# A two-layer graph-attention kernel: where three steps at the start stand, and how the last pairs' units are shared out

## The chip, the cores and the metric

The kernel runs on one core of one Trainium2 chip (trn2). The metric is the device time of one execution in microseconds, as a median over runs. Everything is float32.

## The reference, cut to what matters

There are 64 graphs of 256 nodes with 512 features each, one adjacency matrix of 256 x 256 for all of them, and two layers with a residual each:

```python
h = relu(layernorm(x))
q, k, v = h @ Wq + bq, h @ Wk + bk, h @ Wv + bv            # 8 heads of 64
s = q k^T / 8 + (1 - adj) * -1e9                           # per head
x = x + (softmax(s) @ v) @ Wo + bo
h = relu(layernorm(x))
g = h @ W
e = leaky_relu(g a1 + (g a2)^T, 0.2) * adj
x = x + elu(softmax(e) @ g + beta * g)
```

## The kernel before, in words

**Pairs and units.** The graphs are worked in 32 pairs (`NP`). A product of a pair with a 512 x 512 weight is done with seven block products instead of eight, in the manner of Strassen and Winograd: two graphs by two halves of the features make the four blocks of one operand, and sums and differences of blocks make up the rest. One such product is a `Unit`; its seven block products are issued by `u.p(i)` in the order 1, 4, 6, 2, 7, 5, 3, and `products(u, ...)` adds the step that writes results: `put11` after p2, `put2` after p5, `put12` after p3. Each block product is eight recorded matmuls on TensorE. Between the products VectorE makes running sums out of PSUM: `u2` after p6 (L262), `u3` after p7 (L265). The units are `UnitQK` (two for each pair, L317), `UnitV` (`v_p`), `UnitO` (`o_p`, the output projection) and `UnitW` (`w_p`, the second layer's weight). `p2` and `p3` add to the banks of p1 and p5, so p3 cannot start before `put2` has read p5's bank.

**Block sums.** Three functions make the sums of the activations that a unit needs: `combine_31` (two of them, on POOL for o in `o_blocks`, L435, on VectorE for h and z), `combine_2` (L281, needed by p6) and `combine_4` (L285, needed by p3). The tiles of o are called s_o in the profile, those of z s_z.

**Layer 0.** `scores(b, q)` makes four heads' scores of graph b on TensorE (L393); ScalarE takes the exponential (L397), POOL multiplies by the mask (L398) and adds the two halves (L400), 128 x 512 and 128 x 256 at a time. `values(b, q)` multiplies by v (`av`, L411), makes the sums of the softmax (`sm`, L420), and VectorE does the reciprocal (L422), adds to a check sum and writes oT (L426 follows on POOL, put off to a later place by `between`). `residuals(p)` loads x again through SyncE's queue into y (L442) and adds bo and a constant on POOL (L443). `UnitO` adds into y.

**Layer 1.** `y_stats`, `y_scales`, `y_normal` make the layer norm into h2; `y_sums` multiplies h2 by two rows derived from W and a (`pr`, L486, on VectorE); `gat_scores` turns the sums into rows on TensorE (`pe`, L160) and makes e; `gat_exp`, `divide`, `gat_t` (transposes `at`, L519, copied to eT at L520), `gat_z` (`pz`, L533), and `UnitW` with elu: m on ScalarE (L553, L554), o on VectorE (L556), and `finish`, which adds m to o on the engine that it is given (L562) and stores it.

**Order.** `tc.manual_schedule` holds TensorE, VectorE, ScalarE and POOL to the order in which the program is written, and each engine's queue runs in that order: an instruction that waits holds all behind it on its engine. The order is written out in `start` (pair 0), `first` (pair 1, first part), `first_half(p)` and `second_half(p, uo)` for pairs 1 to 30, `last` (pair 31's attention, with unit o_30 and w_29) and `end` (the rest: w_30, o_31, w_31). In the middle, one pair of every kind is worked in each round: o of the pair before, w of the one before that, v and qk of the next.

**Buffers.** PSUM has eight banks under one name. SBUF tiles have a tag with a number of buffers:

```python
BUFS = {"set": 13, "qk": 8, "v": 4, "pt": 4, "xt": 4, "y": 8, "e": 2, "eT": 2, "m": 2, "c": 3, "u": 4}
```

`pr` and the o of elu share the three buffers of "c"; h2 has two of 128 x 2 x 512.

**Small setup.** `project_b` loads Wo, makes its four sums (L116 to L119), and adds bv @ Wo to bo: four columns of bv spread over 128 x 128 (`bvb`, L176, two buffers) and 16 recorded matmuls (`pbo`, L179). It is called between v_0's p5 and p3. `project_a` does the same kind of thing for W; its last part is the product `pwa` (L160).

Of the kernel before, what the change touches and what calls it, by code (L numbers as in the profile page):

```python
# [16 lines left out]
P = 128  # L17
# [6 lines left out]
def kernel(ctx: ExitStack, tc: tile.TileContext, x, adj, wq, bq, wk, bk, wv, bv, wo, bo, w, a, beta, out):  # L24
# [33 lines left out]
    BUFS = {"set": 13, "qk": 8, "v": 4, "pt": 4, "xt": 4, "y": 8, "e": 2, "eT": 2, "m": 2, "c": 3, "u": 4}  # L58
# [103 lines left out]
    def project_b():  # L162

        WO, b12, sums = weight("wo", wo, True)
        sums()
        nc.sync.dma_start(bo2, bo.partition_broadcast(P))
        bvc = sb([P, DC], "bvc", "bvc", 1)
        with nc.allow_non_contiguous_dma(reason="a bias, once"):
            bv_v = bv.rearrange("(q i s d) -> i d q s", q=2, i=4, s=2, d=HH)
            for i in range(4):  # L170
                for q in range(2):
                    nc.sync.dma_start(bvc[i * HH:(i + 1) * HH, 2 * q:2 * q + 2], bv_v[i, :, q, :])
        ps = bank("pbo")
        for c in range(DC):
            cb = sb([P, P], "rec", f"bvb_{c}")
            nc.vector.tensor_scalar(cb, ones, bvc[:, c:c + 1], None, ALU.mult)  # L176
            for f in range(2):
                b = ((WO[1], b12), (WO[2], WO[3]))[c // 2][f]
                nc.tensor.matmul(ps[:, f * N:(f + 1) * N], cb, b[:, c % 2, :], start=(c == 0 and f == 0),  # L179
                                 stop=(c == DC - 1), skip_group_check=True)  # L180
        nc.vector.scalar_tensor_tensor(bo2, bo2, -1.0, ps, op0=ALU.add, op1=ALU.add)
        return WO
# [256 lines left out]
    def residual(p, gi, fh):  # L439
        g = 2 * p + gi  # L440
        r = Y[g, fh] = blk("y", f"y_{g}_{fh}")
        nc.sync.dma_start(r, x[g].rearrange("(t p) c -> p t c", p=P)[:, :, fh * N:(fh + 1) * N])  # L442
        nc.gpsimd.tensor_tensor(r, r, bo2[:, fh * N:(fh + 1) * N].unsqueeze(1).to_broadcast([P, 2, N]), ALU.add)  # L443
# [31 lines left out]
    def normal(g, rstd, nmr):  # L475
        h2 = H2[g] = sb([P, NT, D], "h2", f"h2_{g}")
        SC[g] = sb([P, NT, 2], "s12", f"s12_{g}", 3)
        for t in range(NT):
            for f in range(2):
                nc.scalar.activation(h2[:, t, f * N:(f + 1) * N], Y[g, f][:, t, :], AF.Relu, bias=nmr[:, t:t + 1],  # L480
                                     scale=rstd[:, t:t + 1])

    def node_sums(g, t):
        for j in range(2):
            pr = sb([P, D], "c", f"pr_{g}_{t}_{j}", BUFS["c"])
            nc.vector.scalar_tensor_tensor(pr, H2[g][:, t, :], 1.0, war[:, j, :], op0=ALU.mult, op1=ALU.mult,  # L486
                                           accum_out=SC[g][:, t, j:j + 1])
# [33 lines left out]

    def gat_z(p):
        s = blocks(("z", p), f"z{p}")
        pss = {}
        for gi in range(2):
            g = 2 * p + gi
            h2, eT = H2.pop(g), ET.pop(g)
            for half in range(2):
                ps = pss[gi, half] = bank(f"pz_{g}_{half}")
                for f in range(2):  # L530
                    fs = slice((2 * half + f) * P, (2 * half + f + 1) * P)
                    for k in range(NT):
                        nc.tensor.matmul(ps[:, f * N:(f + 1) * N], h2[:, k, fs], eT[:, k, :],  # L533
                                         start=(k == 0), stop=(k == NT - 1))
                dst = blk("set", f"z_{g}_{half}")
                nc.scalar.copy(dst, two(ps))  # L536
                s[BLOCK[2 * gi + half]] = dst
# [4 lines left out]
        combine_31(s, of(pss[1, 0]), of(pss[1, 1]))  # L542

    class UnitW(Unit):
# [5 lines left out]
        def elu(self, gi, fh, src, o=None):  # L550
            g = 2 * self.pair + gi
            m = blk("m", f"m_{g}_{fh}")
# [22 lines left out]
        def put12(self):  # L575
            nc.vector.tensor_tensor(two(self.b), two(self.b), self.u2, ALU.add)
            self.elu(0, 1, two(self.b))

# [51 lines left out]
    def residuals(p):  # L630
        for gi, fh in ((0, 0), (1, 1), (1, 0), (0, 1)):
            residual(p, gi, fh)
# [6 lines left out]
    def start():  # L639
# [36 lines left out]
        products(uv, 4, 6, 2, 7, 5)  # L676
        wo_blocks = project_b()
# [3 lines left out]
    def first():  # L681
# [37 lines left out]
        products(uv, 6)  # L719
        combine_2(A["o", 0])  # L720
        products(uv, 2)
        x_normals(2, *range(2 * NT))
        products(uv, 7)
        combine_4(A["o", 0])
        products(uv, 5)
        prods(5)
        products(uv, 3)
        uo = UnitO(0)
# [39 lines left out]
    def second_half(p, uo):  # L768
# [37 lines left out]
        scores(g1 + 1, 0, {1: add})  # L806
        residuals(p)
# [5 lines left out]
        products(uv, 4, 6, 2)  # L813
        if p == NP - 2:
            o_blocks(p, "xt")
        products(uv, 7, 5)
        if p == NP - 2:
            combine_24(A["o", p])
# [4 lines left out]
    def last():  # L823
        p = NP - 1
        g0, g1 = 2 * p, 2 * p + 1
        uo = UnitO(p - 1)
        products(uo, 1, 4, 6, 2)
        y_stats_0(p - 1)
        products(uo, 7, 5)
        add = values(g0, 0)  # L830
        y_stats_1(p - 1)
        products(uo, 3)
        y_stats_2(p - 1)
        scores(g0, 1, {0: lambda: y_scales(p - 1), 1: add})
        uw = UnitW(p - 2)
        products(uw, 1, 4)
        y_normal(p - 1, 1)
        products(uw, 6)
        y_sums(p - 1, 1, 0, 1)
        products(uw, 2)  # L840
        y_normal(p - 1, 0)
        products(uw, 7)
        add = values(g0, 1)
        y_sums(p - 1, 0, 0, 1)
        scores(g1, 0, {1: add})
        gat_scores(g1 - 2)
        gat_exp(g1 - 2)
        uw.p(5)
        gat_scores(g0 - 2)
        gat_exp(g0 - 2)  # L850
        uw.put2()
        uw.finish(0, 0, nc.gpsimd)
        divide(p - 1)
        uw.finish(1, 1, nc.vector)
        products(uw, 3)
        uw.finish(1, 0, nc.vector)
        add = values(g1, 0)
        scores(g1, 1, {1: add})
        uw.finish(0, 1, nc.vector)
        residuals(p)  # L860
        gat_t(g1 - 2)
        gat_t(g0 - 2)
        gat_z(p - 1)
        values(g1, 1)()
        o_blocks(p)

    def end():
        p = NP - 1
        g0, g1 = 2 * p, 2 * p + 1
        z = A["z", p - 1]  # L870
        uw = UnitW(p - 1)
        products(uw, 1, 4)
        combine_24(A["o", p])
        uo = UnitO(p)
        products(uo, 1, 4, 6, 2, 7)
        combine_24(z)
# [5 lines left out]
        normal(g1, rstd, minus(mr, f"y{g1}"))  # L882
        products(uw, 6)
        products(uo, 3)
        y_stats(g0, NT, 0, g0, 1)
        rstd, mr = scales(f"y{g0}", 2)
        y_sums(p, 1, 0, 1)
        products(uw, 2)
        normal(g0, rstd, minus(mr, f"y{g0}"))
        products(uw, 7)  # L890
# [3 lines left out]
        uw.p(5)  # L894
# [3 lines left out]
        gat_t(g1)  # L898
        uw.put2()
        uw.finish(0, 0, nc.gpsimd)  # L900
        gat_divide(ATT[g0], gsums[:, NT * g0:NT * g0 + NT], g0)
        products(uw, 3)
        uw.finish(1, 1, nc.gpsimd)
        gat_t(g0)
        uw.finish(1, 0, nc.gpsimd)
        gat_z(p)
        uw.finish(0, 1, nc.gpsimd)
# [4 lines left out]
        products(uw, 3)  # L912
        uw.finish(1, 1, nc.vector)
        uw.finish(1, 0, nc.gpsimd)
        uw.finish(0, 1, nc.vector)

    with tc.manual_schedule(engines={ENG.PE, ENG.DVE, ENG.Activation, ENG.Pool}):
# [4 lines left out]
        for p in range(2, NP - 1):  # L922
            second_half(p, first_half(p))
        last()
# [31 lines left out]
    def general(src, dst, W, mask):  # L956
# [77 lines left out]
        for f in range(DC):  # L1034
            ps = bank(f"fz_{f}")
            for k in range(NT):
                nc.tensor.matmul(ps[:, :N], h2[:, k, f * P:(f + 1) * P], eT[:, k, :], start=(k == 0),
# [65 lines left out]
```

## Time and profile before

| | |
|---|---|
| median of 3 runs | 2902.8 us (2901.25 to 2905.18) |
| profiled execution, its own time | 2903.83 us |
| its span | 2902.0 us, clock 0.99 |
| TensorE busy | 2852.2 us, 98% |
| VectorE busy | 2063.2 us, 71% |
| POOL busy | 1618.4 us, 56% |
| ScalarE busy | 1046.3 us, 36% |
| one pair in the middle | 88.1 us |
| TensorE without a stop | 175.5 to 2763.5 us |
| TensorE's last product ends | 2892.35 us |

In the profile PE is TensorE, DVE VectorE, ACT ScalarE, POOL GpSimd, SP SyncE. A row of the timeline gives the start, the length, the engine and line, the operation, its output and inputs and, in brackets, how long the engine stood idle before it and what ended that. Matmuls that follow each other without a gap share a row. A line of the waits gives engine, line, what was waited for, and then total us, times and the longest.

### The profile page before, as it was taken

The numbers are of one execution on the slowest core, as the hardware profiler recorded it, in microseconds if no ns is written. First come the engines' busy times: TensorE is split into PE (matmuls) and PEld (weight loads), VectorE is DVE, ScalarE is ACT, GpSimd is POOL, SyncE is SP. The second block draws the span as 40 slices with busy tenths as digits, with TensorE's granted clock in tenths as the row PEclk, the third lists the DMA queues.
The fourth block names the chain that finished last, engine by engine and source line by source line (L and its number), as shares of the span: only waits on it lengthen the run. The fifth ranks groups of instructions, "written<-read, shape, count | busy, mean of one in ns | idle before, by whom it ended". The sixth has DMA issues, their size and how long they took to land.

```text
span 2902.0 us, 46357 instructions
## 1 busy us (share of the span) xinstructions
PE 2852.2 (98%) x18110; PEld 2338.2 (81%) x18110; DVE 2063.2 (71%) x3652; ACT 1046.3 (36%) x2116; POOL 1618.4 (56%) x1588
## 2 busy tenths in 40 slices
PE   8899999999999999999999999999999999999987
PEld 7688888888888888888888888888888888888865
DVE  5567767677767678666677676777676786666765
ACT  2233333334333334333333333343333343333332
POOL 2656555556555565555565555565555655555752
PEclk9999999999999999999999999999999999999998
DMA  5001111001110011110011110011110111100110
GB/s 152 9 15 44 44 45 44 16 30 44 45 44 32 21 37 45 44 44 26 19 44 44 45 44 15 30 45 44 44 32 21 37 44 44 45 26 19 30 30 30
DMA packets 96463, 110.00 MB, mean 38 GB/s; under 512 B 8560, under 2 KB 79472, under 8 KB 96240
## 3 DMA queue, kind: packets, MB, share of 16 engines
q1 hardware_dynamic: 96240, 106.99, 11.8%
q8 instruction: 145, 2.38, 0.4%
q14 instruction: 78, 0.64, 0.1%
HBM read 73.41 MB, written 33.55 MB: 37 GB/s over the span
## 4 chain that ended last, share of the span: by engine, by line
PE 96%; DVE 2%; POOL 1%; issue 0%; ACT 0%; DMA 0%; SPq 0%; DVEq 0%; POOLq 0%; ACTq 0%
PE qk_p L329 27%; PE v_p L362 14%; PE o_p L362 13%; PE w_p L362 13%; PE sc L393 8%; PE av L411 8%; PE pz L533 8%; PE tr L308 2%; PE sm L420 2%; PE at L519 1%; PE pe L160 0%; POOL pt L398 0%; DVE pr L486 0%; PE pbo L179 0%; DMA x<-in_x_dram 0%
## 5 line engine op out<-in xcount | busy, mean ns | idle before, releaser
L398 POOL TENSOR_TENSOR pt<-pt,maskT 128x512 f32<-128x512 f32 x512 | 719.5, 1405 | 601.1 <-ACT pt L397 601.1
L400 POOL TENSOR_TENSOR pp<-pt 128x256 f32<-128x256 f32 x512 | 433.6, 847 | 40.1
L397 ACT ACTIVATE pt<-sc 128x512 f32<-128x512 f32 x512 | 264.4, 603 | 344.9 <-PE sc L393 344.7
L486 DVE SCALAR_TENSOR_TENSOR pr<-h,war 128x512 f32<-128x512 f32 x256 | 303.3, 1228 | 57.2 <-ACT h L480 57.2
L562 POOL TENSOR_TENSOR o<-o,m 128x512 f32<-128x512 f32 x36 | 45.9, 1276 | 512.1 <-ACT m L554 471.1
L393 PE MATMUL sc<-qk 64*128 64x256 f32 x2048 | 255.7, 389 | 0.0
L411 PE MATMUL av<-pt,v 128*32 128x256 f32 x4096 | 250.2, 383 | 2.4 <-POOL pt L398 2.4
L393 PEld LDWEIGHTS sc<-qk 64*128 64x128 f32 x2048 | 187.3, 186 | 69.9 <-PE av L411 37.9
L422 DVE RECIPROCAL rec<-sm 128x256 f32<-128x256 f32 x128 | 223.3, 1745 | 14.5 <-PE sm L420 14.5
L533 PE MATMUL pz<-eT,h 128*128 128x256 f32 x1024 | 228.9, 382 | 2.8 <-ACT eT L520 2.8
L533 PEld LDWEIGHTS pz<-eT,h 128*128 128x128 f32 x1024 | 196.2, 192 | 30.5 <-ACT eT L520 3.4
L411 PEld LDWEIGHTS av<-pt,v 128*32 128x32 f32 x4096 | 120.6, 110 | 112.7 <-issue 33.5
L329 PE MATMUL qk_p<-s_h,wq_t 128*128 128x256 f32 x768 | 197.4, 379 | 0.0
L329 PE MATMUL qk_p<-s_h,wk_t 128*128 128x256 f32 x768 | 197.1, 379 | 0.0
L362 PE MATMUL w_p<-w_t,s_z 128*128 128x256 f32 x768 | 177.9, 381 | 0.0
L362 PE MATMUL v_p<-wv_t,s_h 128*128 128x256 f32 x768 | 176.3, 379 | 0.0
L362 PE MATMUL o_p<-wo_t,s_o 128*128 128x256 f32 x768 | 176.3, 379 | 0.0
L540 DVE TENSOR_TENSOR s_z<-pz,z 128x512 f32<-128x512 f32 x64 | 44.2, 691 | 179.1 <-ACT z L536 179.1
L536 ACT COPY z<-pz 128x512 f32<-128x512 f32 x128 | 74.9, 585 | 254.1 <-PE pz L533 254.1
L362 PEld LDWEIGHTS w_p<-w_t,s_z 128*128 128x128 f32 x768 | 146.6, 191 | 20.1
L362 PEld LDWEIGHTS o_p<-wo_t,s_o 128*128 128x128 f32 x768 | 145.8, 190 | 20.1 <-ACT pt L397 0.3
L362 PEld LDWEIGHTS v_p<-wv_t,s_h 128*128 128x128 f32 x768 | 145.8, 190 | 20.1 <-ACT pt L397 0.3
(167 smaller groups left out, 5728.6 us busy)
## 6 DMA issues: line engine op xcount, KB each, us to landing
x<-in_x_dram SPq DMA_DIRECT2D x128, 256.0 KB, 3.7
y<-in_x_dram SPq DMA_DIRECT2D x128, 256.0 KB, 2.9
out_dram<-o SPq DMA_DIRECT2D x128, 256.0 KB, 2.2
wq_b<-in_L_gnn_Wq_dram SPq DMA_DIRECT2D x4, 256.0 KB, 5.7
wk_b<-in_L_gnn_Wk_dram SPq DMA_DIRECT2D x4, 256.0 KB, 6.2
wv_b<-in_L_gnn_Wv_dram SPq DMA_DIRECT2D x4, 256.0 KB, 5.0
wo_b<-in_L_gnn_Wo_dram SPq DMA_DIRECT2D x16, 64.0 KB, 2.1
w_b<-in_L_gnn_W_dram SPq DMA_DIRECT2D x4, 256.0 KB, 3.4
```

Of the source, the lines that this page charges most:

```text
L308: nc.tensor.transpose(ps[:, c * N + t * P:c * N + (t + 1) * P], XT[g, t][:, f0:f0 + P], ident)
L329: nc.tensor.matmul(ps[:, j * N:(j + 1) * N], wj[i][:, c, ft * P:(ft + 1) * P], s[i][:, c, :], start=(start and j == 0 and c == 0), stop=(c ...
L362: nc.tensor.matmul(ps[:, t * N:(t + 1) * N], s[i][:, c, t * P:(t + 1) * P], wj[i][:, c, :], start=(start and t == 0 and c == 0), stop=(c = ...
L393: nc.tensor.matmul(pss[2 * pair + h][:, k * N:(k + 1) * N], qk[hs, 1, k * P:(k + 1) * P], qk[hs, 0, :], start=True, stop=True)
L397: nc.scalar.activation(pt, two(pss[i]), AF.Exp, scale=QSCALE)
L398: nc.gpsimd.tensor_tensor(pt, pt, maskT, ALU.mult)
L400: nc.gpsimd.tensor_tensor(pp, pt[:, 0, :], pt[:, 1, :], ALU.add)
L411: nc.tensor.matmul(ps[i * HH:(i + 1) * HH, s * N:(s + 1) * N], v[:, k, c0:c0 + HH], pts[i][:, k, :], start=(k == 0), stop=(k == NT - 1))
L422: nc.vector.reciprocal(rec, sums[:, :N])
L486: nc.vector.scalar_tensor_tensor(pr, H2[g][:, t, :], 1.0, war[:, j, :], op0=ALU.mult, op1=ALU.mult, accum_out=SC[g][:, t, j:j + 1])
L533: nc.tensor.matmul(ps[:, f * N:(f + 1) * N], h2[:, k, fs], eT[:, k, :], start=(k == 0), stop=(k == NT - 1))
L536: nc.scalar.copy(dst, two(ps))
```

## The change

Five edits.

1. `project_b` is cut in two calls. The Wo sums are issued after v_0's p6 instead of after p5; the four bvb columns (`shift(0)`) after p7, in two tiles of two columns; the pbo products (`shift(1)`) stay after p5.
2. In `first`, combine_2 and combine_4 of o_0 move from between v_1's products to behind its p3.
3. The end. In `second_half(30)` o_blocks is issued ahead of the residuals, and gat_z(29), v_31's p3 and the combines go into `last`. There, values and scores of pair 31 are put between the parts of units o_30 and w_29; all of o_31 comes in `end`, ahead of the z product of pair 30 and unit w_30; `divide(30)` is later; pair 31's residuals and h2 take buffers of "qk"; more of the finishes are on POOL.
4. w_31's last block (`put12_finish`) is done in two halves, each 128 x 256, with two stores.
5. h2 is two tiles of 128 x 512 with four buffers; `gat_z` is cut into a function for each graph.

```diff
         ps = bank("pbo")
-        for c in range(DC):
-            cb = sb([P, P], "rec", f"bvb_{c}")
-            nc.vector.tensor_scalar(cb, ones, bvc[:, c:c + 1], None, ALU.mult)
-            for f in range(2):
-                b = ((WO[1], b12), (WO[2], WO[3]))[c // 2][f]
-                nc.tensor.matmul(ps[:, f * N:(f + 1) * N], cb, b[:, c % 2, :], start=(c == 0 and f == 0),
-                                 stop=(c == DC - 1), skip_group_check=True)
-        nc.vector.scalar_tensor_tensor(bo2, bo2, -1.0, ps, op0=ALU.add, op1=ALU.add)
-        return WO
+        cbs = []
+
+        def part(n):
+            if n == 0:
+                for c in range(DC):
+                    if c % 2 == 0:
+                        cbs.append(sb([P, 2, P], "rec", f"bvb_{c}"))
+                    nc.vector.tensor_scalar(cbs[-1][:, c % 2, :], ones, bvc[:, c:c + 1], None, ALU.mult)
+                return
+            for c in range(DC):
+                for f in range(2):
+                    b = ((WO[1], b12), (WO[2], WO[3]))[c // 2][f]
+                    nc.tensor.matmul(ps[:, f * N:(f + 1) * N], cbs[c // 2][:, c % 2, :], b[:, c % 2, :],
+                                     start=(c == 0 and f == 0), stop=(c == DC - 1), skip_group_check=True)
+            nc.vector.scalar_tensor_tensor(bo2, bo2, -1.0, ps, op0=ALU.add, op1=ALU.add)
+
+        return WO, part
...
-    def residual(p, gi, fh):
+    def residual(p, gi, fh, tag):
         g = 2 * p + gi
-        r = Y[g, fh] = blk("y", f"y_{g}_{fh}")
+        r = Y[g, fh] = blk(tag, f"y_{g}_{fh}")
...
-    def normal(g, rstd, nmr):
-        h2 = H2[g] = sb([P, NT, D], "h2", f"h2_{g}")
+    def normal(g, rstd, nmr, tag="h2"):
+        h2 = H2[g] = [sb([P, D], tag, f"h2_{g}_{t}", BUFS[tag]) for t in range(NT)]
...
+    def z_graph(p, gi):
+        s = A.get(("z", p)) or blocks(("z", p), f"z{p}")
+        h2, eT = H2.pop(2 * p + gi), ET.pop(2 * p + gi)
+        s["ps"] = []
+        for half in range(2):
+            ps = bank(f"pz_{p}_{gi}_{half}")
+            s["ps"].append(ps)
+            for f in range(2):
+                fs = slice((2 * half + f) * P, (2 * half + f + 1) * P)
+                for k in range(NT):
+                    nc.tensor.matmul(ps[:, f * N:(f + 1) * N], h2[k][:, fs], eT[:, k, :],
+                                     start=(k == 0), stop=(k == NT - 1))
+            dst = s[BLOCK[2 * gi + half]] = blk("set", f"z_{p}_{gi}_{half}")
+            nc.scalar.copy(dst, two(ps))
+
...
+        def put12_finish(self):
+
+            g = 2 * self.pair
+            y, m, o = Y.pop((g, 1)), blk("pt", f"m_{g}_1"), blk("pt", f"o_{g}_1")
+            for t in range(NT):
+                src = self.b[:, t * N:(t + 1) * N]
+                nc.vector.tensor_tensor(src, src, self.u2[:, t, :], ALU.add)
+                nc.scalar.activation(m[:, t, :], src, AF.Relu, scale=-1.0)
+                nc.scalar.activation(m[:, t, :], m[:, t, :], AF.Exp, scale=-1.0)
+                nc.vector.scalar_tensor_tensor(o[:, t, :], src, 0.0, y[:, t, :], op0=ALU.max, op1=ALU.add)
+            for t in range(NT):
+                nc.vector.tensor_tensor(o[:, t, :], o[:, t, :], m[:, t, :], ALU.add)
+                nc.sync.dma_start(out[g, t * P:(t + 1) * P, N:], o[:, t, :])
...
-        products(uv, 4, 6, 2, 7, 5)
-        wo_blocks = project_b()
+        products(uv, 4, 6)
+        wo_blocks, shift = project_b()
+        products(uv, 2, 7)
+        shift(0)
+        products(uv, 5)
+        shift(1)
         products(uv, 3)
...
         o_blocks(0)
         residuals(0)
-        products(uv, 6)
-        combine_2(A["o", 0])
-        products(uv, 2)
+        products(uv, 6, 2)
         x_normals(2, *range(2 * NT))
-        products(uv, 7)
-        combine_4(A["o", 0])
-        products(uv, 5)
+        products(uv, 7, 5)
         prods(5)
         products(uv, 3)
+        combine_24(A["o", 0])
         uo = UnitO(0)
...
+        if p == NP - 2:
+            o_blocks(p, "xt")
         residuals(p)
         uv = UnitV(p + 1)
         uv.p(1)
         gat_t(g1 - 2)
         gat_t(g0 - 2)
         products(ub, 3)
-        products(uv, 4, 6, 2)
+        products(uv, 4, 6, 2, 7, 5)
         if p == NP - 2:
-            o_blocks(p, "xt")
-        products(uv, 7, 5)
-        if p == NP - 2:
-            combine_24(A["o", p])
+            return uv
         gat_z(p - 1)
         products(uv, 3)
         combine_24(A["z", p - 1])
-    def last():
+    def last(uv):
         p = NP - 1
         g0, g1 = 2 * p, 2 * p + 1
+        combine_24(A["o", p - 1])
+        add = values(g0, 0)
+        scores(g0, 1, {1: add})
+        products(uv, 3)
         uo = UnitO(p - 1)
-        products(uo, 1, 4, 6, 2)
+        products(uo, 1, 4, 6, 2, 7)
         y_stats_0(p - 1)
-        products(uo, 7, 5)
-        add = values(g0, 0)
+        add = values(g0, 1)
+        scores(g1, 0, {1: add})
+        products(uo, 5)
         y_stats_1(p - 1)
+        gat_z(p - 2)
         products(uo, 3)
         y_stats_2(p - 1)
-        scores(g0, 1, {0: lambda: y_scales(p - 1), 1: add})
+        y_scales(p - 1)
+        combine_24(A["z", p - 2])
+        add = values(g1, 0)
+        scores(g1, 1, {0: lambda: y_normal(p - 1, 1), 1: add})
+        residuals(p, "qk")
         uw = UnitW(p - 2)
         products(uw, 1, 4)
-        y_normal(p - 1, 1)
+        y_sums(p - 1, 1, 0, 1)
         products(uw, 6)
-        y_sums(p - 1, 1, 0, 1)
-        products(uw, 2)
         y_normal(p - 1, 0)
-        products(uw, 7)
-        add = values(g0, 1)
-        y_sums(p - 1, 0, 0, 1)
-        scores(g1, 0, {1: add})
+        products(uw, 2, 7)
         gat_scores(g1 - 2)
         gat_exp(g1 - 2)
         uw.p(5)
+        add = values(g1, 1)
+        o_blocks(p)
+        add()
+        uw.finish(0, 0, nc.gpsimd)
+        uw.put2()
+        y_sums(p - 1, 0, 0, 1)
+        uw.finish(1, 1, nc.vector)
+        products(uw, 3)
+        uw.finish(1, 0, nc.gpsimd)
+        combine_24(A["o", p])
         gat_scores(g0 - 2)
         gat_exp(g0 - 2)
-        uw.put2()
-        uw.finish(0, 0, nc.gpsimd)
-        divide(p - 1)
-        uw.finish(1, 1, nc.vector)
-        products(uw, 3)
-        uw.finish(1, 0, nc.vector)
-        add = values(g1, 0)
-        scores(g1, 1, {1: add})
-        uw.finish(0, 1, nc.vector)
-        residuals(p)
-        gat_t(g1 - 2)
-        gat_t(g0 - 2)
-        gat_z(p - 1)
-        values(g1, 1)()
-        o_blocks(p)
+        uw.finish(0, 1, nc.gpsimd)
     def end():
         p = NP - 1
         g0, g1 = 2 * p, 2 * p + 1
-        z = A["z", p - 1]
-        uw = UnitW(p - 1)
-        products(uw, 1, 4)
-        combine_24(A["o", p])
         uo = UnitO(p)
-        products(uo, 1, 4, 6, 2, 7)
-        combine_24(z)
+        products(uo, 1, 4, 6)
+        divide(p - 1)
+        products(uo, 2, 7)
         y_stats(g0, NT, 0, g0, 0)
         products(uo, 5)
         y_stats(g1, NT, 0, g1, 1)
         y_stats(g1, NT, 0, g1, 0)
         rstd, mr = scales(f"y{g1}", 2)
-        normal(g1, rstd, minus(mr, f"y{g1}"))
-        products(uw, 6)
         products(uo, 3)
         y_stats(g0, NT, 0, g0, 1)
+        gat_t(g1 - 2)
+        gat_t(g0 - 2)
+        normal(g1, rstd, minus(mr, f"y{g1}"), "qk")
         rstd, mr = scales(f"y{g0}", 2)
+        gat_z(p - 1)
+        normal(g0, rstd, minus(mr, f"y{g0}"), "qk")
         y_sums(p, 1, 0, 1)
-        products(uw, 2)
-        normal(g0, rstd, minus(mr, f"y{g0}"))
-        products(uw, 7)
+        combine_24(A["z", p - 1])
+        uw = UnitW(p - 1)
+        products(uw, 1, 4, 6)
         gat_scores(g1)
         gat_exp(g1)
         y_sums(p, 0, 0, 1)
-        uw.p(5)
+        products(uw, 2, 7)
         gat_divide(ATT[g1], gsums[:, NT * g1:NT * g1 + NT], g1)
         gat_scores(g0)
         gat_exp(g0)
-        gat_t(g1)
-        uw.put2()
+        products(uw, 5)
         uw.finish(0, 0, nc.gpsimd)
         gat_divide(ATT[g0], gsums[:, NT * g0:NT * g0 + NT], g0)
+        uw.finish(1, 1, nc.gpsimd)
         products(uw, 3)
-        uw.finish(1, 1, nc.gpsimd)
+        uw.finish(1, 0, nc.gpsimd)
+        gat_t(g1)
         gat_t(g0)
-        uw.finish(1, 0, nc.gpsimd)
+        uw.finish(0, 1, nc.gpsimd)
         gat_z(p)
-        uw.finish(0, 1, nc.gpsimd)
         combine_24(A["z", p])
         uw = UnitW(p)
         products(uw, 1, 4, 6, 2, 7, 5)
         uw.finish(0, 0, nc.gpsimd)
-        products(uw, 3)
-        uw.finish(1, 1, nc.vector)
+        uw.finish(1, 1, nc.gpsimd)
+        uw.p(3)
+        uw.put12_finish()
         uw.finish(1, 0, nc.gpsimd)
-        uw.finish(0, 1, nc.vector)
```

## The prediction

> **What bounds the kernel now.** I read the page's busy shares first, then its slices, the chain, TensorE's waits, and the timelines of the two ends.
>
> ```profile
> PE 2852.2 (98%) x18110; PEld 2338.2 (81%) x18110; DVE 2063.2 (71%) x3652; ACT 1046.3 (36%) x2116; POOL 1618.4 (56%) x1588
> ...
> PE   8899999999999999999999999999999999999987
> ...
> PEclk9999999999999999999999999999999999999998
> ...
> PE 96%; DVE 2%; POOL 1%; issue 0%; ACT 0%; DMA 0%; SPq 0%; DVEq 0%; POOLq 0%; ACTq 0%
> ```
>
> TensorE is busy for 98% of the span and makes 96% of the chain; its row and its clock row fall below 9 only at the two ends. The table of stretches (PE busy and count are the first pair after the length, PEclk is the column before the DMA share) says how sharp that is:
>
> ```profile
> 175.50:2663.60 2488.10, 2488.10 (x15935) 2046.39 (x15934) 1799.94 (x3167) 919.95 (x1866) 1426.73 (x1388) 1.00 0.12 36
> 2763.50:2775.00 11.50, 11.50 (x73) 9.55 (x75) 5.84 (x10) 0.58 (x1) 0.00 (x0) 1.00 0.01 1
> 2775.00:2800.00 25.00, 22.64 (x153) 15.89 (x146) 18.37 (x35) 10.19 (x20) 13.35 (x14) 0.93 0.04 11
> 2800.00:2830.00 30.00, 20.70 (x153) 14.38 (x152) 21.83 (x35) 10.69 (x24) 22.65 (x21) 0.83 0.20 62
> 2842.00:2870.00 28.00, 18.94 (x67) 13.31 (x66) 25.66 (x63) 11.93 (x28) 7.88 (x10) 0.78 0.08 29
> 2870.00:2890.00 20.00, 19.82 (x82) 16.66 (x81) 5.05 (x8) 4.16 (x7) 1.96 (x2) 0.88 0.04 14
> ```
>
> From 175.5 us on TensorE never stops for 2488.10 us, at clock 1.00. Two things follow. A wait taken out before 175.5 moves everything behind it, one for one. And nothing on the other engines is worth anything in the middle. What can be had is what TensorE's waits name:
>
> ```profile
> PE v_p L362 <- DVE v L379: 11.5, 1, 11.5
> PE pe L160 <- DVE pr L486: 7.9, 6, 2.5
> PE w_p L362 <- DVE o L570: 7.1, 3, 4.8
> PE pbo L179 <- issue: 4.2, 1, 4.2
> PE pz L533 <- ACT eT L520: 2.8, 2, 1.5
> PE av L411 <- POOL pt L398: 2.4, 2, 2.2
> ```
>
> (total us, times, longest). The first and the fourth lie at the start, the rest in the last 130 us. A stop also costs clock: eight recorded matmuls of a block product take 1.73 us at full speed, and 3.78 after a long stop.
>
> **The change, part by part.**
>
> *Weight sums of Wo (project_b).* TensorE ends v_0's p5 at 49.47. VectorE then does v's put2 (49.50 to 50.71), four sums of 0.61 and two bvb columns; pbo starts at 53.62, after 4.15 idle, and its 16 matmuls take 6.23 instead of 16 x 0.216 = 3.46: 2.77 of slow clock. So 6.9 us lie there. The change puts the sums behind v_u (L262, ended 45.08), ahead of p7's L265 (possible at 47.78), and the four columns ahead of put2. Their loads were issued by 29.7, so no transfer is in the way. Uncovered, sums of 0.61 end at 47.5, the columns (0.24 each) at 49.4: no stop, 6.9 won. But POOL multiplies the masked scores until 48.65, and a VectorE operation with two SBUF inputs beside POOL is slow here:
>
> ```profile
> 2786.14 1.14 DVE L486 SCALAR_TENSOR_TENSOR pr<-h,war 128x512 f32<-128x512 f32 x1
> ...
> 2788.34 1.75 DVE L486 SCALAR_TENSOR_TENSOR pr<-h,war 128x512 f32<-128x512 f32 x1
> ...
> 2851.78 0.69 DVE L486 SCALAR_TENSOR_TENSOR pr<-h,war 128x512 f32<-128x512 f32 x1
> ```
>
> The first two ran beside POOL, the third with POOL idle. The Trainium skill (SBUF — State Buffer, "SBUF: two separate sides") has the rule that speaks against this edit: such an operation and one of GpSimd hold a shared port pair exclusively, and the loser waits the whole instruction out. By the bare 0.61 the gain is 6.9; by the rule, with the rows beside it (about 1.2 each), the sums end at 49.9, L265 at 50.5, the columns at 51.5: a stop of 2.0 remains, 2.15 is won, and of the 2.77 slow clock I give half (1.4). I take 3.5; ends 1.5 (POOL's products delayed in their turn, up to 0.6) and 6.9.
>
> *combine_2/combine_4 of o_0 behind v_1.* VectorE's queue stands in an order, and s2_o (L281) waits in it:
>
> ```profile
> 124.05 1.73 DVE L281 TENSOR_TENSOR s_o<-s_o,oT 128x512 f32<-128x512 f32 x1 [12.34 <-POOL s_o L435]
> ...
> 128.11 3.78 PE L362 MATMUL v_p<-wv_b,s_h 128*128 128x256 f32 x8 [11.46 <-DVE v L379]
> ```
>
> POOL makes s_o at 121.54 to 124.02, behind the products of scores(2,0). Behind L281 stand v's L265 and put2 (L379), and for L379 waits TensorE's last product of v_1. Cost: 11.46 idle, 2.05 on that product (3.78 against 1.73), 1.23 on o_0's p1 (2.96 against 1.73): 14.7. With both combines behind v_1's p3, put2 follows p5 at once, and p3 can start at 116.65. What is late next: TensorE does p3, o_0's p1 and p4 (to 121.9), values(2,0) (2.3, its last POOL product ready at 121.54), scores(2,1) (1.93), and at 126.1 wants s2_o for p6. VectorE can start s2_o at 124.05, takes 1.73 beside POOL's residuals, and the hop is 0.1 to 0.3: 0 to 1.2 of wait. Then values(2,1) wants POOL's products of scores(2,1), which stand behind the four residuals (to 129.81) and take 4 x 2.03: 137.9 at the last sum, against about 136.5: 1.2 more. I take 2.4 of new waits, none long enough to slow the clock: gain 12.3. Ends 10 (both doubled) and 14.7.
>
> *The tail.* From 2763.4 TensorE's own work at full speed is 92.3 us (five units of 12.1, three rounds of values and scores at 4.2, two z products at 6.9, the rest 5); it took until 2892.35, 129.0. So 36.7 are lost: 21.3 in recorded stops, the other 15.4 in slow clock. The clock column agrees: 0.07 x 25 + 0.17 x 30 + 0.22 x 28 + 0.12 x 20 = 15.4. The change moves gat_z(29), the last product of v_31 and scores into this stretch as cover, puts all of unit o_31 ahead of w_30, and sends finishes to POOL. I laid both orders out, every engine's queue in its written order, each instruction with its duration from this trace. The large stops left in the new order:
>
> w_29's p3: it needs put2, which stands on VectorE behind values(63,1): after `sm` come rec 1.66, acc 0.3, oT 0.61, put2 0.61 and a hop, 3.5. Before: 4.82. The pe stop of graph 60: pr needs one of three "c" buffers, the first held by o_58_0, whose finish is on POOL behind four residuals and o_blocks (6 x 1.24, and acc 0.7), 1.27 itself, then its store (2.2), then four pr of 0.61 to 0.7: 7.2 in two pieces, against 3.25. Three of 1 each (o_31's p1, its p3, the first z product), from VectorE's chain. Around w_30: s2_z 1.2, pe of graph 62 1.1 (was 0.50 and 0.90), w_30's p3 3.2 (was 1.56), the transposes 1.15, pz_31 2.8 (was 1.53). w_31's p3 0.9. Gone: av <- pt 2.36, pe of graph 63 3.2. Sum: 24.2 idle. The same laying-out gives 28 for the old order where the trace has 21.3, so I scale: 24.2 x 21.3 / 28 = 18.4.
>
> For the slow clock the rule is the Trainium skill's (TensorE: Matmul & The Clock Gate, "What's actually happening"): half rate after an idle window of about 3.4 us, and again for as long before it is released. The trace is harsher:
>
> ```profile
> 2819.69 7.17 PE L533 MATMUL pz<-eT,h 128*128 128x256 f32 x32 [1.23 <-ACT eT L520]
> ...
> 2869.66 9.67 PE L533 MATMUL pz<-eT,h 128*128 128x256 f32 x32 [1.53 <-ACT eT L520]
> ```
>
> Full speed is 6.9: after 1.23 idle next to nothing, after 1.53 (with smaller stops just before) 2.8. By the rule only stops over 3.4 count: one before (4.82), two after (3.5 and the pe stop), so the slow clock would grow by 1.7. By the trace six stops of 1.5 or more carry 15.4, 2.6 each; four of that size after give 10.3. The measurement decides: 18.4 + 10.3 = 28.7 against 36.7, gain 8.0. Ends: 2 with the idle unscaled (24.2 + 10.3), and 18 if the pe stop of 7.2 is covered and its clock with it (28.7 - 7.2 - 2.6 = 18.9 lost).
>
> *The last block in halves.* Before, p3 ends at 2892.35 and the last addition at 2897.02: relu waited 1.49 for a buffer of m, then 0.63 + 0.63 + 0.61 + 0.61. In halves, with m and o in "pt", four half steps and half additions take about 2.9, but POOL's finish(1,0) (two of 1.27 in a row) ends 2.1 to 2.4 after p3 and its store follows. Gain 0.7; ends 0 (the final store sets the end either way: 4.98 from the last addition to the span's end) and 1.6.
>
> *h2 as two tiles.* The same bytes and order on each engine in the middle; a few waits more on the queues, beside a TensorE that never stops. Cost 0; without cover up to 0.1 a pair, 3 us.
>
> Sum: 3.5 + 12.3 + 8.0 + 0.7 = 24.5. The profiled execution took 2903.8, 1.0 above the median of 2902.8; 2903.8 - 24.5 = 2879.3, and at the median 2878.3. I say 2879.
>
> **The rivals.**
>
> *The tail gives nothing.* POOL has four residuals, two o_blocks and the finishes in one row there, and VectorE is 25.66 of 28 busy around w_30 already. If new stops eat the cover, only the start is won: 2903 - 16 = 2887, reaching to 2891 with both start terms at their low ends. For it: the 7.2 of the pe stop. Against: av <- pt and the w_30 chain are shortened by work that is really there. Chance 0.22.
>
> *The covers hold.* The pe stop hidden and the sums free of POOL: 6.9 + 13 + 14 + 1 = 35, 2868. For it: my layout puts more idle than the trace shows. Against: the o_58_0 chain is one behind the other. Chance 0.17.
>
> *A wait in the middle (slower).* One mechanism: gat_z's eight h2 loads per graph now depend on two tiles with buffers of their own, and pz is on the path. If a pair's chain slips by d us in each of 30 pairs, the loss is 30 d; it cancels 24 at d = 0.8 and at d = 1.1 gives 2911. Nothing in TensorE's waits between 175.5 and 2763.5 points to it, since there are none. Chance 0.04.
>
> *The start does not move.* The pbo stop stays because the sums wait for POOL, and a new wait at o_0's p6 eats the rest: 2903 - 8 - 6 = 2889 or so. Chance 0.05.
>
> **How the numbers follow.** The likeliest case (0.52) gives 2879, its own range 2873 to 2885. The first rival adds to 2891, the second to 2868; beyond these lies about 0.15. Range 2868 to 2890. A measurement of this kernel tells about 0.2% (5.8 us) from no change. Faster by more than that: all but the slower rival and a sliver, 0.95; same 0.02; slower 0.03.
>
> **What would show it.** Right: no TensorE wait over 1.5 between 110 and 140; pbo's stop about 2; the middle still without a stop; pe of graph 60 the largest stop of the tail; TensorE's last product about 24 earlier. Wrong: any stop between 175 and 2740; pbo's stop still 4; a tail with more than 22 us of stops, or fewer than 12.

## The result and the profile after

The kernel after takes 2878.8 us (median of 4 runs, 2878.5 to 2880.3) against 2902.6 before: ratio 0.9918 (0.9901 to 0.9935), 23.8 us faster. The forecast was 2879. Its profiled execution has a span of 2876.8 us; that of before had 2902.0.

The page of the kernel after, busy shares and the two rows of slices:

```profile
PE 2841.9 (99%) x18110; PEld 2332.8 (81%) x18110; DVE 2062.8 (72%) x3652; ACT 1046.2 (36%) x2118; POOL 1620.4 (56%) x1591
...
PE   9999999999999999999999999999999999999987
...
PEclk9999999999999999999999999999999999999989
```

Every engine does the same work as before. TensorE's 18110 instructions are busy for 10.3 us less, mostly because fewer of them run at a slow clock. The first two slices of PE now read 9, and the end still falls off. The stretches of the kernel after (PE busy and count follow the length, PEclk stands before the DMA share):

```profile
164.00:2651.00 2487.00, 2487.00 (x15928) 2045.74 (x15928) 1794.45 (x3156) 919.02 (x1861) 1425.43 (x1385) 1.00 0.12 36
...
2775.00:2800.00 25.00, 15.37 (x85) 11.10 (x84) 17.97 (x31) 7.86 (x17) 17.44 (x17) 0.70 0.09 32
2800.00:2820.00 20.00, 18.48 (x83) 15.54 (x83) 14.27 (x32) 5.68 (x14) 3.38 (x7) 0.94 0.04 13
2820.00:2845.00 25.00, 16.53 (x77) 12.95 (x75) 20.55 (x46) 10.53 (x25) 3.85 (x4) 0.97 0.09 32
```

The middle has no stop, as before. What is lost at the end is now gathered in one place, 2775 to 2800, where TensorE is busy for 15.37 of 25 us. TensorE's waits after (total us, times, longest):

```profile
PE pe L160 <- DVE pr L494: 7.1, 3, 5.3
PE w_p L370 <- DVE o L581: 6.8, 3, 3.4
PE pz L540 <- ACT eT L528: 3.1, 2, 2.4
PE at L527 <- DVE e L518: 2.2, 1, 2.2
PE pbo L186 <- issue: 1.7, 1, 1.7
...
PE av L419 <- POOL pt L406: 0.6, 1, 0.6
```

The line that led before, v_p waiting 11.5 us for v, is gone. pbo's stop is 1.7 instead of 4.2. The pe, w_p and pz waits of the end are nearly as long in sum as they were.

The times of three instructions that both kernels have split the 25.2 us between the two spans. v_0's p4 starts 0.67 earlier after (39.90 against 40.57), which is no part of the change. From there to v_0's p3 it is 14.17 us instead of 19.12: 4.95 from the Wo sums. From there to the middle (the transposes of one pair, 1538.22 against 1556.98, where the lead is 18.76): 13.14 from the combines. Up to the start of w_31's p3 (2866.25 against 2890.53) the lead grows by 5.52: the new order of the end. From there to the end of the span it is 10.55 instead of 11.47: 0.92 from the halves. Sum: 0.67 + 4.95 + 13.14 + 5.52 + 0.92 = 25.2.

### The profile page after: what moved, and what is told of

Read it like the earlier page. It is cut to its first block, busy times and chain, and to the rows that moved or that the text cites. A ratio compares the mean times of both kernels' runs of the same rounds, so it can differ in the third digit from the quotient of the medians.

```text
span 2876.8 us, 46368 instructions
## 1 busy us (share of the span) xinstructions
PE 2841.9 (99%) x18110; PEld 2332.8 (81%) x18110; DVE 2062.8 (72%) x3652; ACT 1046.2 (36%) x2118; POOL 1620.4 (56%) x1591
## 4 chain that ended last, share of the span: by engine, by line
## 5 line engine op out<-in xcount | busy, mean ns | idle before, releaser
L370 PEld LDWEIGHTS w_p<-w_t,s_z 128*128 128x128 f32 x768 | 145.7, 190 | 21.1 <-issue 1.5
```

The lines of the kernel that those rows point to most:

```text
L370: nc.tensor.matmul(ps[:, t * N:(t + 1) * N], s[i][:, c, t * P:(t + 1) * P], wj[i][:, c, :], start=(start and t == 0 and c == 0), stop=(c = ...
```

## The experiments

### The parts, each alone

The Wo sums in the kernel before:

```diff
-        products(uv, 4, 6, 2, 7, 5)
-        wo_blocks = project_b()
+        products(uv, 4, 6)
+        wo_blocks, shift = project_b()
+        products(uv, 2, 7)
+        shift(0)
+        products(uv, 5)
+        shift(1)
```

> The kernel before with the first edit alone (Wo's sums after v_0's p6, the four bvb columns after p7, pbo after p5). Theory (the parts add up, and the traces of before and after show each one's share): the pbo stop falls from 4.15 to about 1.7, the slow clock on pbo goes, 5.0 us faster than before, about 2897.7. Rival (the prediction's smaller share, 3.5, and the rest of the start belongs to the combines): 2899. Rival (the sums beside POOL delay POOL's products, and the gain is given back at values(0,0)): 2901 or more.

Measured: 2897.7 against 2902.8 in the same series, ratio 0.9983 (0.9976 to 0.9989): 5.1 faster. The profile of the whole change shows how it goes. The four sums and the columns on VectorE, and pbo on TensorE, in the timeline of the kernel after:

```profile
44.34 1.37 DVE L116 TENSOR_TENSOR wo_t<-wo_b,wo_b 128x512 f32<-128x512 f32 x1
45.74 1.10 DVE L117 TENSOR_TENSOR wo_t<-wo_b,wo_t 128x512 f32<-128x512 f32 x1
46.76 1.75 DVE L118 TENSOR_TENSOR wo_t<-wo_b,wo_b 128x512 f32<-128x512 f32 x1
48.44 1.21 DVE L119 TENSOR_TENSOR wo_t<-wo_b,wo_t 128x512 f32<-128x512 f32 x1
...
50.54 3.69 PE L186 MATMUL pbo<-wo_b,bvb 128*128 128x256 f32 x16 [1.74 <-issue]
```

The sums take 1.10 to 1.75 each beside POOL's products instead of 0.68, and POOL's last product in turn 1.72 instead of 1.27. The stop that is left is 1.74. After it pbo runs at nearly full speed: 3.69, where it took 6.23 after a stop of 4.15. The slow clock that the edit takes away differs between executions: in the profiles of the combines alone and of the end alone, which have the old order here, pbo took 5.38 behind the same 4.15. From v_0's p4 to its p3 the six profiles with the old order take 18.27 to 19.57, the four with the sums in this place 14.15 to 14.17.

The combines of o_0 in the kernel before:

```diff
-        products(uv, 6)
-        combine_2(A["o", 0])
-        products(uv, 2)
+        products(uv, 6, 2)
...
-        products(uv, 7)
-        combine_4(A["o", 0])
-        products(uv, 5)
+        products(uv, 7, 5)
         prods(5)
         products(uv, 3)
+        combine_24(A["o", 0])
```

> The kernel before with the second edit alone (combine_2 and combine_4 of o_0 behind v_1's p3). Theory: the stop of 11.46 at v_1's p3 is VectorE's queue held by s2_o, and goes with its slow clock; 13.1 us faster, about 2889.5, with a wait of under 1.3 left at values(2,1). Rival (the stop only moves to o_0's p6 and to values(2,1), as the prediction's lower end has it): 10 faster, 2892.6.

Measured: 2889.7, ratio 0.9956 (0.9942 to 0.9969): 13.0 faster. From the timeline of the kernel after, the instruction that held the queue and the product that waited for it:

```profile
110.97 1.99 PE L370 MATMUL v_p<-wv_b,s_h 128*128 128x256 f32 x8
...
118.53 1.74 DVE L289 TENSOR_TENSOR s_o<-s_o,oT 128x512 f32<-128x512 f32 x1 [4.83 <-POOL s_o L443]
```

VectorE still waits for POOL's s_o, 4.83 us. Nothing on TensorE's path is behind it any more: p3 has no bracket, so it did not wait.

A rival way to the same end leaves the combines where they are and moves POOL's part instead, so that s_o is ready in time:

```diff
         add = values(1, 1)
+        o_blocks(0)
         x_scales(2)
         scores(2, 0, {1: add})
-        o_blocks(0)
```

> The kernel before with o_blocks(0) ahead of scores(2,0), so that POOL makes s_o before the eight products of scores(2,0) and not after; the combines stay between v_1's products. Theory (the 11.46 stop is s_o's place in POOL's queue, handed on by VectorE's order): s_o is ready about 8 us earlier, the stop at v_1's p3 is under 1, POOL's products come 2.5 later and values(2,0) waits about 2: 11 to 13 us faster than before, 2890 to 2892. Rival (VectorE cannot finish v_1's put2 in time anyhow, with x's statistics and the pwa copies around it): the stop stays above 5, 2896 or more.

Measured: 2889.4, ratio 0.9955 (0.9942 to 0.9969), 13.4 faster, the same as the edit. Its timeline:

```profile
112.38 0.69 DVE L281 TENSOR_TENSOR s_o<-s_o,oT 128x512 f32<-128x512 f32 x1 [0.53 <-POOL s_o L435]
...
122.57 1.70 PE L411 MATMUL av<-pt,v 128*32 128x256 f32 x25 [0.93 <-POOL pt L398]
```

VectorE's wait falls from 12.34 to 0.53 with L281 in its old place, and TensorE's 11.46 with it. So the stop was the late s_o, handed on by VectorE's order; it can be cut at either end. The price was as expected in kind, a wait for POOL's delayed product at values(2,0), but 0.93 and not 2.

The end with the halves and the h2 tiles, the first two edits undone (the diff is edits 3 to 5 of the change):

> The kernel after with the first two edits undone: the end's new order, the last block in halves and h2 in two tiles. Theory (traces): the end gains 5.5 and the halves 0.9, so 6.4 faster than before, about 2896.2, with the same stops as the kernel after (pe of graph 60 5.3 and 0.9, w_29's p3 3.4). Rival (the prediction's 8.0 + 0.7, and the rest lost by chance in the one profile): 2893.9.

Measured: 2896.6, ratio 0.9977 (0.9967 to 0.9986), 6.2 faster. In its profile w_29's p3 waits 3.38, as expected, but pe of graph 60 waits 6.50 and 0.93 instead of 5.3 and 0.9. The three parts measured alone come to 5.1 + 13.0 + 6.2 = 24.3, and the change as a whole to 23.8: they add up.

The halves alone:

```diff
-        products(uw, 3)
-        uw.finish(1, 1, nc.vector)
+        uw.finish(1, 1, nc.gpsimd)
+        uw.p(3)
+        uw.put12_finish()
         uw.finish(1, 0, nc.gpsimd)
-        uw.finish(0, 1, nc.vector)
```

> The kernel before with w_31's last block in two halves alone (and its finish(1,1) on POOL). Theory: 0.9 us faster, about 2901.7, which is within what can be told from no change; the profile's distance from the start of w_31's p3 to the span's end falls from 11.47 to about 10.5. Rival (the last store sets the end whatever is done before it): no change, distance 11.4.

Measured: 2902.4, ratio 0.9998 (0.9989 to 1.0006). By the time alone this is open. The distance from w_31's p3 to the span's end is 10.5 in its profile. Over all profiles of this study it is 10.5 to 11.2 in the nine with the halves and 11.3 to 11.8 in the five without, in the mean 0.7 less. That speaks for a gain of 0.7 to 0.9.

h2 in two tiles alone:

```diff
-        h2 = H2[g] = sb([P, NT, D], "h2", f"h2_{g}")
+        h2 = H2[g] = [sb([P, D], "h2", f"h2_{g}_{t}", BUFS["h2"]) for t in range(NT)]
```

> The kernel before with h2 in two tiles of 128 x 512 (four buffers) alone. Theory (no cost: TensorE never stops in the middle): 2902.8, within 0.5. Rival (the slower case of the prediction: more waits on the z products, up to 0.1 us a pair): up to 3 slower, 2905.8, and a stop of TensorE in the middle.

Measured: 2902.7 against 2903.2 beside it, ratio 0.9998 (0.9990 to 1.0006), and in its profile TensorE is busy for 2487.00 us of 2487.00 from 176 on. No cost.

### What is left of pbo's stop

In the kernel after, the sums are moved further up, to where POOL has no products yet:

```diff
         x_normals(1, *range(2 * NT))
+        wo_blocks, shift = project_b()
         uv.p(1)
...
-        products(uv, 4, 6)
-        wo_blocks, shift = project_b()
-        products(uv, 2, 7)
+        products(uv, 4, 6, 2, 7)
```

> The kernel after with Wo's four sums moved further up, behind the layer norm of pair 1 and ahead of v_0's p1, where POOL has no products yet; the bvb columns and pbo stay. Theory (what is left of the pbo stop, 1.74, is the sums' 1.10 to 1.75 each beside POOL's products): the sums take 0.61 to 0.7 each, the stop at pbo goes, nothing else in the start stops, 1.7 to 3.4 us faster than the kernel after, 2875.4 to 2877. Rival (VectorE simply has too much to do between p6 and p5, whoever it runs beside): a new stop of the same 2 us at qk or v_0's first products, 2878.8.

Measured: 2879.5 (2878.2 to 2880.1): by the time nothing was won, as the rival has it. The profile speaks against the rival. Its new stop of 2 us did not come: pbo had no stop, and v_0's p4 to p3 took 12.19 us instead of 14.17. But p4 started at 41.92 and not at 39.90: VectorE waited another 0.63 us for an x tile of pair 0, the transposes of its second graph began at 10.30 instead of 9.96, and the first two groups of qk took 1.91 and 1.51 us instead of 1.03. That lies in the first 16 us, ahead of anything moved, and so both kernels were run once more, side by side:

> The kernel after itself, beside the next one on the same chip, because the first 12 us differ by up to 2 us between profiles (v_0's p4 started at 39.90 in the kernel after and at 41.92 in the run with the sums moved up). Both theories: 2878.8, between 2878 and 2880.5.

> Wo's sums ahead of v_0's p1, as before, again and beside the kernel after. Theory (the missing gain was the first 12 us of those executions, an x load landing late and slow clock behind it): 1.5 to 2.5 faster than the kernel after beside it, about 2876.8. Rival (the moved sums themselves cost as much somewhere in the start or the end): no difference, 2879.

Measured: 2878.7 (2877.5 to 2880.2) and 2876.7 (2876.6 to 2877.8): 2.0 us apart. Timelines of the second run with the sums moved up:

```profile
35.97 0.68 DVE L116 TENSOR_TENSOR wo_t<-wo_b,wo_b 128x512 f32<-128x512 f32 x1
...
48.40 3.62 PE L186 MATMUL pbo<-wo_b,bvb 128*128 128x256 f32 x16
```

A sum takes 0.68 here and pbo does not wait. The four sums took 5.43 beside POOL and take 2.74 here; the difference is more than the 1.74. So the stop was the sums' time beside POOL. In the one profile of the first series the granted clock was half from 11.4 to 14.9 us, ahead of anything that the edit moves; that the other four executions of that series had the same is likely from their times, but not shown.

### The stops of the end

pe of graph 60 is the longest stop of the kernel after (5.33 and then 0.93). Its pr waits for a buffer that the store of o_58_0 holds, and the store follows the finish on POOL:

```profile
2789.77 1.26 POOL L573 TENSOR_TENSOR o<-o,m 128x512 f32<-128x512 f32 x1
...
2793.29 1.36 DVE L494 SCALAR_TENSOR_TENSOR pr<-h,war 128x512 f32<-128x512 f32 x1 [0.58 <-DMA out_dram<-o]
```

Ahead of that finish on POOL stand pair 31's residuals, 2781.75 to 2786.69, then o_blocks and acc. Here the residuals are issued earlier:

```diff
+        residuals(p, "qk")
         products(uo, 5)
...
         scores(g1, 1, {0: lambda: y_normal(p - 1, 1), 1: add})
-        residuals(p, "qk")
```

> The kernel after with pair 31's four residuals issued ahead of o_30's p5 instead of behind scores(63,1): they leave POOL's queue ahead of o_blocks, acc and the finish of o_58_0. Theory (the pe stop of graph 60, 5.33 + 0.93, is POOL's queue: 4.94 of residuals stand ahead of the finish and of the sum that VectorE's check waits for): the stop falls by 2 to 4, time 2 to 3 faster than the kernel after, 2876 to 2877. Rival (VectorE is the limit of this stretch, 17.97 busy of 25 and in order): the stop turns up elsewhere between o_31's p1 and the z product, 2878.8.

Measured: 2878.1 (2877.0 to 2879.7), 0.6 to 0.7 less than the kernel after, not to be told apart by the times. Its profile has the pe stop at 3.47 instead of 5.33 (6.05 in the repetition of the kernel after). From v_0's p3 to w_31's p3 it takes 2810.63 us; the four profiles that have the kernel after's code in this stretch take 2811.45 to 2812.72, so the gain there is 0.8 to 2.1 in this one profile. The stop shrank as expected, and the time by less than expected. The profile shows one reason. POOL, free of the residuals, now waits for VectorE before its second block sum, and the finish of o_58_0 starts only 1.1 us earlier than before (2788.66):

```profile
2786.75 1.27 POOL L443 TENSOR_TENSOR s_o<-oT,oT 128x512 f32<-128x512 f32 x1 [2.85 <-DVE oT L433]
```

All of that together, and the finish of o_58_0 ahead of o_blocks:

```diff
         add = values(g1, 1)
+        uw.finish(0, 0, nc.gpsimd)
         o_blocks(p)
         add()
-        uw.finish(0, 0, nc.gpsimd)
         uw.put2()
...
-        combine_24(A["o", p])
         gat_scores(g0 - 2)
+        combine_24(A["o", p])
         gat_exp(g0 - 2)
```

> The kernel after with Wo's sums ahead of v_0, pair 31's residuals ahead of o_30's p5, the finish of o_58_0 ahead of o_blocks on POOL, and combine_2 and combine_4 of o_31 behind gat_scores(60) on VectorE. Theory (the three stops have three causes, and each goes by its own edit): 3 from the start, 2 to 3 from the residuals, 1 to 2 from the finish and up to 1 from the combines: 7 to 9 faster than the kernel after, 2870 to 2872. Rival (the end is bound by VectorE's own work and only the start's share comes): 2876.

Measured: 2873.6 (2873.4 to 2873.6), ratio to the kernel before 0.9899 (0.9884 to 0.9914), 5.2 us less than the kernel after, which ran in other series against the same kernel before. It beats both kernels. From v_0's p3 to w_31's p3 it takes 2809.18, 3.0 less than the kernel after (2.3 to 3.5 less than the four profiles named above), and v_0's p4 to p3 12.19, 1.98 less. I had expected 7 to 9 and the end gave 3 instead of 4 to 6.

Why the end gives so little shows when its largest single stop is taken away. In this best version w_29's put2 goes ahead of values(63,1):

```diff
         uw.p(5)
-        add = values(g1, 1)
         uw.finish(0, 0, nc.gpsimd)
+        uw.put2()
+        add = values(g1, 1)
         o_blocks(p)
         add()
-        uw.put2()
-        y_sums(p - 1, 0, 0, 1)
+        y_sums(p - 1, 0, 0, 1, tag="v")
```

> The best version so far (Wo's sums early, residuals early, the finish ahead of o_blocks, combines of o_31 later) with w_29's put2 also ahead of values(63,1) on VectorE, and pr of graph 60 in buffers of v. It takes away the stop of 3.38 at w_29's p3 with its 2.05 of slow clock. Theory (VectorE works through one row of steps here, and TensorE must wait for the whole of it somewhere): the stop turns up at pe of graph 60 as 5 or more, time within 1.5 of the best version, 2872 to 2874. Rival (each stop is a cost of its own): 5 faster, 2868.5.

Measured: 2873.9 (2871.3 to 2874.7), no different. TensorE's stops in the best version, and then in this one:

```profile
2784.99 3.78 PE L370 MATMUL w_p<-w_b,s_z 128*128 128x256 f32 x8 [3.38 <-DVE o L581]
2790.64 0.45 PE L160 MATMUL pe<-ident,s 128*128 128x128 f32 x1 [1.87 <-DVE pr L494]
2792.01 0.48 PE L160 MATMUL pe<-ident,s 128*128 128x128 f32 x1 [0.93 <-DVE pr L494]
```

```profile
2790.30 0.29 PE L160 MATMUL pe<-ident,s 128*128 128x128 f32 x1 [4.50 <-DVE pr L494]
2793.01 0.48 PE L160 MATMUL pe<-ident,s 128*128 128x128 f32 x1 [2.41 <-DVE pr L494]
```

The 3.38 is gone, and the two pe stops grew from 2.80 to 6.91. The second pe comes at 2792.01 in one and at 2793.01 in the other; counted from v_0's p3, which came 2.2 later in the second profile, that is 1.2 earlier. VectorE has a row of steps to work through here, and TensorE waits for the end of it, in two stops or in three. The row itself also grew: the four pr now run while POOL works, and take 0.68, 1.74, 1.20 and 1.74, where they took 0.68, 1.62, 0.69 and 0.69. So this run does not tell what the stop would be worth with the row unchanged. From v_0's p3 to w_31's p3 it took 2807.41, 1.8 less than the best version; a small part of the stop may have been won, but the times do not show it.

## Why the prediction was right, point by point

**Wo sums: 3.5 forecast, 5.1 measured.** The stop was forecast at 2.0 and is 1.74. The rule of the shared port pair (the Trainium skill, SBUF — State Buffer, "SBUF: two separate sides") decided it, with this case's durations: the sums took 5.4 us in all where the bare 0.61 would have had 2.4. Mis-sized was the clock: I had left half of the 2.77 in place, and almost none was left. How much there is to lose varies: pbo's 5.38 in two other profiles had 1.9 of it.

**Combines: 12.3 forecast, 13.0 measured.** The new waits were forecast at 1.2 for o_0's p6 and 1.2 for values(2,1). p6 has none (s2_o ended at 120.27, p6 began at 120.57), and values(2,1) waits 0.59. Nothing slowed the clock.

**The end: 8.0 forecast, 5.5 in the profile.** The named stops are the ones that came, and where:

| stop | forecast | measured |
|---|---|---|
| w_29's p3 | 3.5 | 3.37 |
| pe of graph 60 | 7.2 | 5.33 + 0.93 |
| o_31's p1, its p3, first z product | 1 each | 0, 0.79, 0.73 |
| s2_z of w_30 | 1.2 | 1.09 |
| pe of graph 62 | 1.1 | 0.84 |
| w_30's p3 | 3.2 | 2.74 |
| transposes of graph 62 | 1.15 | 2.15 |
| pz_31 | 2.8 | 2.37 |
| w_31's p3 | 0.9 | 0.72 |

Their sum is 21.1, just inside the 22 that I had named as a sign of being wrong. The sizes differ between executions: in the repetition pe of graph 60 waited 6.05 and 0.93, the transposes 0.48. The laying-out had 24.2, and I had scaled that to 18.4 by the error of the same laying-out on the old order. This scaling failed, by 2.7. With it goes the reason that I gave for the gain: the stops were 21.3 before and are 21.1 after, so the cover shortened them by 0.2 and not by 2.9.

What the new order won is mostly clock. The loss to slow clock can be measured: it is half of TensorE's busy time in the stretches where the granted clock is 0.50. Before, there are four such stretches at the end, from 2792.8 us on, with 21.0 us of busy time: 10.5 lost. After, there are two, 2785.3 to 2802.3 and 2843.3 to 2850.1, with 14.1: 7.0 lost. So 3.5 came from the clock, where 5.1 was forecast (15.4 to 10.3). The other profiles say the same: the six with the old order of the end have 21.0 to 21.5 us idle there and 9.7 to 10.6 lost to the clock, the five with the new order 20.3 to 21.2 and 6.2 to 8.0. Of the 5.5 us, 0.2 are stops, 3.5 clock, and 1.8 lie in neither; what they are stays open.

My 15.4 was no measurement of the clock but what the stops left of the 36.7. The clock column seemed to confirm it because I multiplied by the whole stretches, with the idle time in them. With TensorE's busy time from the same rows (22.64, 20.70, 18.94 and 19.82) the sum is 11.7. And 2.6 for each stop of 1.5 or more, four after, is not what happened: there were five such stops. That the clock term came near is in part luck.

**Halves: 0.7 forecast, 0.9 in the profile, 0.7 in the mean of all profiles. h2: 0 and 0.**

The errors had both signs: 1.6 and 0.7 too little at the start, 2.5 too much at the end. So the total fell on the mark more closely than its terms, and that closeness is luck.

**The rivals.** That the end gives nothing is ruled out by the end alone, whose ratio stays below 0.9986. That the start does not move is ruled out by its two parts alone. The slower case, a wait in the middle through the h2 tiles, does not exist: the interval of h2 alone ends at 1.0006, which is 1.7 us, and the middle has no stop. That all covers hold was wrong twice: the pe stop came, and the sums of Wo were slow beside POOL.

**The clock rule.** I read the trace as harsher than the Trainium skill's rule (TensorE: Matmul & The Clock Gate, "What's actually happening"), and charged every stop of 1.5 or more. The runs do not bear that out: a single stop of 1.74 ahead of pbo cost no clock. Nor do they bear out a bound at 3.4: stops of 3.37 (at w_29's p3) and even 2.75 were followed by slow clock. The last section has the rest.

## What to carry to other kernels

When one engine is the bound everywhere but at the ends, list its stops and ask of each which queue hands the delay on: an instruction that waits in an in-order queue for a late producer can be moved behind what the bound engine needs, or its producer can be moved up, and here both gave 13 us. A stop that comes from a whole row of steps on another engine mostly changed its place here when one step was moved; taking steps out of that row, or off that engine, is the next thing to try, and was not tried. A stop has two prices, the idle time and the slow clock behind it, and an order can win in one without the other: measure both. When two parts of a few us are to be compared, measure from an instruction behind the start-up to one ahead of the end: the first 16 us of this kernel differed by as much as the effect.

## What the runs showed of the hardware that was not expected

The slow clock after a stop is not a function of the stop. w_30's p3 stands behind the same stop in these three profiles, of the kernel after, of its repetition and of the first run with the sums moved up:

```profile
2837.92 1.99 PE L370 MATMUL w_p<-w_b,s_z 128*128 128x256 f32 x8 [2.74 <-DVE o L581]
```

```profile
2837.40 3.31 PE L370 MATMUL w_p<-w_b,s_z 128*128 128x256 f32 x8 [2.75 <-DVE o L581]
```

```profile
2837.86 3.58 PE L370 MATMUL w_p<-w_b,s_z 128*128 128x256 f32 x8 [2.74 <-DVE o L581]
```

After 2.74 to 2.75 idle the same eight matmuls took 1.99, 3.31 and 3.58. The granted clock was 1.00 through the first, and 0.50 from 2837.9 to 2841.3 in the second and from 2837.7 to 2841.1 in the third. The same section of the skill says that the gate watches a window of about 3.4 us that runs freely. The traces agree: in all 14 profiles every stretch between two changes of the granted clock is a whole multiple of 3.41 us (5, 12, 2 and 6 of them at the end of the kernel after).

The traces also show what in a window counts. Lay windows of 3.41 us on these changes and take TensorE's busy share of each. Over all 14 profiles, without the windows at full clock that were busy for 97% and more, this comes out:

| granted clock in the window | busy share | clock in the next window |
|---|---|---|
| 1.00 | up to 0.44 | 0.50, in all 49 |
| 1.00 | 0.45 to 0.51 | 0.50 in 3, 1.00 in 3 |
| 1.00 | 0.52 and more | 1.00, in all 96 |
| 0.50 | up to 0.77 | 0.50, in all 72 |
| 0.50 | 0.78 to 0.82 | 0.50 in 5, 1.00 in 2 |
| 0.50 | 0.83 and more | 1.00, in all 53 |

So in this kernel the clock fell when TensorE was busy for less than about half of one window, and came back after a window that was busy for about four fifths. A window did not have to be idle for the clock to fall after it. The shares are from recorded busy times, whose ends are modelled. The stop of 2.74 in the first profile fell across a border, in two windows of 0.60 and 0.57; in the other two it fell into one window, of 0.20 and 0.25.

A stop of 3.37 cost 2.05 on the product behind it (3.78 against 1.73), and pz_31, behind two stops of 2.15 and 2.37 with 0.85 of work between, took 9.32 where 6.9 is full speed.

The start of the kernel differs between executions: v_0's p4 began between 39.41 and 42.51 us in the profiles of this study, with the same matmuls ahead of it. In the three that began at 41.92 and later the granted clock was half for one window between 11.4 and 15.7 us; in the other eleven it was full and they began at 39.41 to 40.57. In the one looked into, 0.34 of 2.02 us was a later x tile, and nearly all of the rest was slow clock on the transposes and the first two groups of qk.
